# Attention rows: the two halves of the keys added on VectorE before the denominator matmuls, and the output's statistics taken as sums and squares

## The chip, the cores and the metric

The kernel runs on one core of a Trainium2 chip. Each core has a matrix engine (TensorE, PE in the profile, with its weight loads listed as PEld), an elementwise engine (VectorE, DVE), a function engine (ScalarE, ACT), GpSimd (POOL) and a queue for transfers (SyncE, SP). Each engine works through its own list of instructions in order, and they wait for each other through semaphores. SBUF is the working memory, PSUM the memory that TensorE writes to. The metric is the device time of one execution in microseconds (us), the median over runs.

## The reference

The input x is a 256 x 256 image of 128 channels in float32. Four layers follow each other, each of the form x = x + layer(group_norm(x)): triangle attention, a gated recurrence in a transformed space, a triangle product, and a 3 x 3 convolution. The change lies in layer 0 and in the statistics that layer 1 takes of its output. Layer 0, for every image row i, four heads h of 32 channels, and all j, k from 0 to 255:

```
zn = layer_norm(group_norm(x))
q, k, v = zn @ Wq, zn @ Wk, zn @ Wv;   bias = zn @ Wb;   g = sigmoid(zn @ Wg)
scores[i,j,k,h] = q[i,j,h] . k[i,k,h] / sqrt(32) + bias[j,k,h]
a = softmax of scores over k
o[i,j,h] = sum over k of a[i,j,k,h] * v[i,k,h]
x = x + (g * o) @ Wo
```

The group norm of layer 1 needs the mean and the variance of the new x in groups of four channels over the whole image.

## The kernel before

The image lies transposed in HBM, channels on partitions and pixels along the free dimension (`xT`, `x1T`, ...). `transpose_in` makes it, a first pass in `attention` writes the normalised `znT` and the bias, and `attend_bounded` does the attention. (`attend_any` is another branch for weights too large for an unshifted exponential, and isn't taken for these inputs.)

`attend_bounded` has a loop (L603) of 128 rounds, and each round handles two image rows, a = 2 rp and b = 2 rp + 1. The stages are written out in software-pipelined order: while rows a and b are weighted and summed, the scores of rows a+2 and b+2 are made, the projections of the round after next are made, and the output of the round before is finished. Every operation is pinned to the order in which the source calls it, so each engine's queue is the source's order of its own operations. The steps:

- `project` (L494): `ppq`, `ppk`, `ppv`, `ppg` on TensorE, evacuated by ScalarE to `tq`, `tk`, `tg` and by VectorE to `tv`.
- `score` (L514): q times k for one row, keys on partitions, in two halves of 128 keys (`kc`) and four heads, so the scores come as two PSUM tiles `sc` of 128 x 1024 (two heads each). The `sc` tag has two buffers, and one row uses both.
- `biased` (L528): VectorE adds the bias `bT` to one `sc` tile and puts the result in the SBUF tile `e`. This is also what gives the `sc` buffer back.
- `exponent` (L534): ScalarE takes the exponential of `e` in place.
- `values` (L538): TensorE makes the numerators (`nd[:, 0]`, weights `v`) and the denominators (`nd[:, 1]`, weights all ones). Each is a sum over the 256 keys: two accumulating matmuls per head, one for each half. A float32 matmul appears as two records in the profile, so a group of 8 matmuls is 16 records.
- `gated`, `inverse`, `divide` (L549, L555, L560): the denominator is multiplied by 1 + exp(-g) on VectorE (`dn`), inverted on ScalarE by Ln and Exp, and multiplied into the numerator on VectorE (`og`).
- `output` (L568): `px` = Wo times `og` on TensorE; VectorE adds the old x (`xr`) and takes `bn_stats` of the 512 new columns; every second round GpSimd starts the store.

In round 112 `early_statistics` (L115) aggregates the first seven eighths of the statistics, so that `group_affine` (L75) at the head of the recurrence has only the last eighth to aggregate. `group_affine` has a second form, for statistics that are given as sums and as sums of squares about a shift; the triangle stage already uses it. [...]

Of the kernel before, what the change touches and what calls it, by code (L numbers as in the profile page):

```python
# [17 lines left out]
P = 128  # L18
# [12 lines left out]
class Kernel:  # L31
# [245 lines left out]
            W[n] = self.load(pool, I[src], "w2" + n)  # L277
        W["bv"] = self.column(pool, I["L3_conv_bias"], "bv")

    def attention(self, wp, weights, later, xT, x1T, znT, biasD, stats0, stats1):  # L280
        nc, tc, I = self.nc, self.tc, self.i
        w, wb, vb, wo, small = weights
        with ExitStack() as c:
            with ExitStack() as c1:
                ps0 = c1.enter_context(self.pool(name="awq", bufs=2, space=PSUM))
                ab = self.group_affine(wp, ps0, stats0, self.g4, "0")
                lc, cb = self.centering(wp, ps0, ab, "0")

            bias = wp.tile([P, 2, NH, N], F32, name="bias")
# [86 lines left out]
            flag = nc.values_load(small[0:1, 0:1])  # L376
            self.last = {}
            with tc.If(flag > 0) as branch:
                self.attend_bounded(xT, x1T, znT, bias, first, w, wb, vb, wo, stats1)
            self.last = {}  # L380
            with branch.Else():
                self.attend_any(xT, x1T, znT, bias, w, wb, wo, stats1)
            self.last = {}

    def bounded(self, wp, raws, w, wb):
# [64 lines left out]
            V.tensor_copy(fl, top[:, 1:2])  # L450
            return fl

    def attend_bounded(self, xT, x1T, znT, bias, first, w, wb, vb, wo, stats1):


        nc, tc = self.nc, self.tc
# [1 line left out]
        with ExitStack() as c:  # L458
# [17 lines left out]
            pin = lambda f: lambda *a, **k: tc.keep_in_program_order(f(*a, **k))  # L476
            mm, act_t, act_i = pin(self.mm), pin(act), pin(self.act)
            tt, stt, bn = pin(V.tensor_tensor), pin(V.scalar_tensor_tensor), pin(V.bn_stats)
            loaded, t, e, nd, dn, og, x1s = {0: first}, {}, {}, {}, {}, {}, {}

            def chunk(rp):

# [51 lines left out]
            def exponent(i, p2):  # L534
                if 0 <= i < N:
                    act_t(e[i, p2], e[i, p2], AF.Exp, scale=-1.0)

            def values(i):  # L538

                v, r = t[i // 2, "v"], i % 2  # L540
                nd[i] = ps.tile([P, 2, N], F32, name="nd", tag="nd")
                for n in range(2):
                    for kc in range(2):
                        for h in range(NH):
                            hs = slice(h * HD, (h + 1) * HD)
                            lhs = ones if n else v[:, 2 * r + kc, hs]
                            mm(nd[i][hs, n, :], lhs, e[i, h // 2][:, h % 2, kc, :], start=kc == 0, stop=kc == 1)

            def gated(i):  # L549

# [17 lines left out]
            def output(rp):  # L568
                if rp < 0:
                    return  # L570
                xr = chunk(rp)[1]
                if rp % 2 == 0:
                    x1s[rp // 2] = io.tile([P, 1024], F32, name="x1")
                x1 = x1s[rp // 2]
                s = slice((rp % 2) * 512, (rp % 2) * 512 + 512)
                px = ps.tile([P, 512], F32, name="px", tag="pj")
                mm(px, wo["f"], og[rp])
                tt(x1[:, s], px, xr, ALU.add)
                bn(stats1[:, rp, :], x1[:, s])
                if rp % 2 == 1:  # L580
                    nc.gpsimd.dma_start(x1T[:, (rp - 1) * 512:(rp + 1) * 512], x1)

# [18 lines left out]
            for rp in range(N // 2):  # L603
                a, b = 2 * rp, 2 * rp + 1
                score(a + 2)
                inverse(b - 2)
                divide(a - 2)
                biased(a + 2, 0)
                divide(b - 2)
                biased(a + 2, 1)  # L610
                for nm in "qkvg":
                    if nm == "g":
                        exponent(b, 1)
                        exponent(a + 2, 0)
                    project(rp + 2, nm)
                output(rp - 1)
                if rp == N * 7 // 16:
                    self.early_statistics(stats1, "1")
                score(b + 2)
                exponent(a + 2, 1)  # L620
                biased(b + 2, 0)
                exponent(b + 2, 0)
                biased(b + 2, 1)
                values(a)
                gated(a)
                inverse(a)
                values(b)
                gated(b)
            inverse(N - 1)
            divide(N - 2)  # L630
            divide(N - 1)
            output(N // 2 - 1)

    def attend_any(self, xT, x1T, znT, bias, w, wb, wo, stats1):

        nc, tc = self.nc, self.tc
        with ExitStack() as c:
            io = c.enter_context(self.pool(name="a2", bufs=2))
            pj = c.enter_context(self.pool(name="a2w", bufs=2))
            hp = c.enter_context(self.pool(name="a2h", bufs=4))  # L640
            ps = c.enter_context(self.pool(name="a2s", bufs=2, space=PSUM))
            with tc.For_i(0, N // 2) as rp:
                zn = io.tile([P, 512], F32, name="zn2")
                nc.sync.dma_start(zn, znT[:, bass.ds(rp * 512, 512)])
                xr = io.tile([P, 512], F32, name="xr")
                nc.sync.dma_start(xr, xT[:, bass.ds(rp * 512, 512)])
                x1 = io.tile([P, 512], F32, name="x1")
                self.attend(rp, zn, xr, x1, w, wb, wo["h"], bias, pj, hp, ps, stats1)
                nc.sync.dma_start(x1T[:, bass.ds(rp * 512, 512)], x1)
            self.early_statistics(stats1, "1")  # L650

    def attend(self, rp, zn, xr, x1, w, wb, wo, bias, pj, hp, ps, stats1):

# [58 lines left out]
        nc.vector.tensor_tensor(x1, px, xr, ALU.add)  # L712
        nc.vector.bn_stats(stats1[:, bass.ds(rp, 1), :].rearrange("p a b -> p (a b)"), x1)

    def recurrence(self, x1T, x2T, HD_, stats1, stats2, shift2):

# [4 lines left out]
        with ExitStack() as c:  # L723
# [4 lines left out]
            V.tensor_scalar_mul(negid, self.ident, -1.0)  # L728
            gw, gb = {}, {}
            with self.pool(name="rwp", bufs=2, space=PSUM) as ps0:  # L730
                ab, mg, _ = self.group_affine(wp, ps0, stats1, self.g4, "1", True)
                V.tensor_scalar_mul(shift2, mg, -1.0)

                abc = wp.tile([P, 2, 2], F32, name="abc")
                pab = ps0.tile([P, 2, 2], F32, name="pab", tag="gn")
                for half in range(2):
                    for ri in range(2):
                        self.mm(pab[half * HC:(half + 1) * HC, ri, :], self.ident[:, ri * HC:(ri + 1) * HC], ab)
                V.tensor_copy(abc, pab)
                for g, add in (("f", 2.0), ("i", 0.0), ("d", 0.0)):  # L740
                    raw, b0 = W["W" + g], W["b" + g]
                    pb = ps0.tile([P, 2], F32, name="rpb" + g, tag="gn")
                    for half in range(2):
                        hs = slice(half * HC, (half + 1) * HC)
                        for ri in range(2):
                            self.mm(pb[hs, ri:ri + 1], raw[:, ri * HC:(ri + 1) * HC], ab[:, 1:2])
                    gb[g] = wp.tile([P, 2], F32, name="gb" + g)
                    V.scalar_tensor_tensor(gb[g], b0, add, pb, ADD, ADD)
                    gw[g] = wp.tile([P, P], F32, name="gw" + g)
                    V.tensor_scalar_mul(gw[g], raw, ab[:, 0:1])  # L750
# [582 lines left out]
    def run(self, ctx):  # L1333
        nc, tc = self.nc, self.tc
        const = ctx.enter_context(tc.tile_pool(name="const", bufs=1))
        dram = ctx.enter_context(tc.tile_pool(name="dram", bufs=1, space=DRAM))
        image = lambda n: dram.tile([P, NPIX], F32, name=n)
        self.constants(const)
        stats = {n: const.tile([P, NCH, 6], F32, name="stats" + n) for n in "013"}

        stats["2"] = const.tile([P, 2, N // 4], F32, name="stats2")
        shift2 = const.tile([P, 1], F32, name="shift2")
        xT, x1T, x2T, x3T, znT = (image(n) for n in ("xT", "x1T", "x2T", "x3T", "znT"))
        biasD = dram.tile([NH, NPIX], F32, name="biasD")
        HD_ = dram.tile([2, 2 * KS, N, HC], F32, name="HD")
        prodD = image("prodD")
        self.early = {n: [const.tile([P, 2], F32, name=f"early{k}{n}") for k in range(2)] for n in "013"}
        later = ctx.enter_context(self.pool(name="lw", bufs=1))
        with self.pool(name="aw", bufs=1) as wp:
            weights = self.attention_weights(wp)  # L1350
            self.transpose_in(xT, HD_, stats["0"])
            self.attention(wp, weights, later, xT, x1T, znT, biasD, stats["0"], stats["1"])
        self.recurrence(x1T, x2T, HD_, stats["1"], stats["2"], shift2)
        pools = []

        def late():

            if not pools:
                pools.append(ctx.enter_context(self.pool(name="cw", bufs=1, side="right")))
            return pools[0]  # L1360

        self.triangle(x2T, x3T, znT, prodD, stats["2"], shift2, stats["3"], lambda *a: self.transformed_taps(late(), *a))
        self.convolution(x3T, stats["3"], late())
# [58 lines left out]
```

## Time and profile before

The time is 5366.57 us, the median of three runs (5366.4 to 5370.02).

| stretch of the trace, us | what runs | TensorE busy | VectorE busy | ScalarE busy | clock |
|---|---|---|---|---|---|
| 0 to 506 | transposition, first pass of attention | 405.1 | 312.0 | 291.1 | 0.85 |
| 506 to 1882 | `attend_bounded` | 1365.1 | 1040.1 | 959.6 | 0.99 |
| 1882 to 3420 | recurrence | 1472.7 | 1499.4 | 1446.4 | 0.99 |
| 3420 to 5367 | triangle and convolution | 1888.5 | 1154.1 | 882.5 | 0.99 |

Busy time is the time in which an engine had an instruction of its own under way; it says nothing on how well that instruction uses the engine. The clock is the share of full speed that TensorE was granted. An entry such as `[1.22 <-PE px L60]` behind a line of the timeline means that the engine stood idle for 1.22 us before this instruction, and that what it waited for was the write of `px` on TensorE. The trace is in the order of starts; starts of successive instructions on one engine lie closer together than their durations, since they overlap in the pipeline. L60, L54 and L476 are the lines of small helpers which record all matmuls, all activations and the pinned VectorE operations, so the tiles' names tell one from the other.

### The profile page before, as it was taken

How to read it: one execution, taken by the hardware profiler on the slowest of the kernel's cores; microseconds unless marked ns; L12 is line 12 of the kernel's file. 1: busy time of each engine (PE TensorE's matmuls, PEld its weight loads, DVE VectorE, ACT ScalarE, POOL GpSimd, SP SyncE). 2: the span in 40 equal slices, each digit the busy share in tenths (PEclk: the TensorE clock that was granted, in tenths of full speed). 3: DMA queues.
4: the chain of work that ended last, by engine and by line, in shares of the span. 5: the costliest groups of instructions: out<-in, count | busy, mean ns of one | idle time of the engine just before them, and what ended most of it. 6: DMA issues, size and time to landing. Idle time of an engine off the chain costs nothing.

```text
span 5367.2 us, 79719 instructions
## 1 busy us (share of the span) xinstructions
PE 5131.3 (96%) x32117; PEld 2871.9 (54%) x32117; DVE 4005.5 (75%) x5023; ACT 3579.7 (67%) x4923; POOL 267.5 (5%) x488
## 2 busy tenths in 40 slices
PE   5699999999999989999999999899999999999999
PEld 4434555555555533333333333338999954339999
DVE  5666777777777779999999999655334526669886
ACT  4376767777776689999999999784333357772210
POOL 1100000000000000000000000000110010000000
PEclk7799999999999989999999999999999999999999
DMA  8875222222222122222222221577667668864331
GB/s 294 331 267 187 68 80 76 72 80 76 72 76 74 57 76 68 72 68 68 68 72 68 68 68 64 207 283 264 230 234 254 234 248 302 295 228 183 141 130 72
DMA packets 185936, 788.84 MB, mean 147 GB/s; under 512 B 36083, under 2 KB 39432, under 8 KB 136384
## 3 DMA queue, kind: packets, MB, share of 16 engines
q1 hardware_dynamic: 120212, 514.73, 29.3%
q0 software_dynamic: 60416, 268.46, 12.4%
q8 instruction: 256, 4.19, 0.3%
q10 hardware_dynamic: 4936, 0.50, 0.1%
q14 instruction: 116, 0.95, 0.1%
HBM read 512.28 MB, written 271.32 MB: 146 GB/s over the span
## 4 chain that ended last, share of the span: by engine, by line
PE 53%; DVE 31%; issue 11%; ACT 2%; DMA 1%; POOL 1%; POOLq 0%; ACTq 0%; DVEq 0%; SPq 0%
PE z L60 9%; PE nd L60 9%; PE m L60 7%; PE sc L60 5%; PE po L60 4%; PE zc L60 4%; DVE tr L796 3%; DVE t L793 3%; DVE y L793 3%; DVE p L793 3%; DVE yf L793 3%; PE ppv L60 3%; PE ppq L60 3%; PE px L60 3%; PE ppk L60 2%
## 5 line engine op out<-in xcount | busy, mean ns | idle before, releaser
L54 ACT ACTIVATE e<-e 128x1024 f32<-128x1024 f32 x512 | 525.4, 1051 | 195.0 <-DVE e L476 194.7
L476 DVE TENSOR_TENSOR e<-sc,bT 128x1024 f32<-128x1024 f32 x512 | 611.5, 1215 | 39.8 <-PE sc L60 39.8
L956 DVE TENSOR_TENSOR LR<-z,sg 128x512 f32<-128x512 f32 x256 | 268.5, 1050 | 363.3 <-ACT sg L54 358.3
L60 PE MATMUL m<-U,v 128*128 128x128 f32 x4608 | 516.5, 276 | 6.6 <-DVE v L1271 6.6
L60 PEld LDWEIGHTS m<-U,v 128*128 128x128 f32 x4608 | 516.4, 192 | 6.7 <-DVE v L1271 6.7
L60 PE MATMUL z<-wf,zt 128*128 128x128 f32 x4096 | 459.5, 275 | 3.6 <-DVE zn L956 3.6
L60 PEld LDWEIGHTS z<-wf,zt 128*128 128x128 f32 x4096 | 459.3, 192 | 4.6 <-DVE zn L956 4.4
L60 PE MATMUL var<-sq,omat 128*128 128x512 f32 x768 | 360.8, 599 | 1.2 <-ACT rs L54 1.2
L54 ACT ACTIVATE dn<-dn 128x256 f32<-128x256 f32 (+1 forms) x640 | 293.8, 459 | 98.6 <-DVE dn L476 88.5
L54 ACT ACTIVATE sg<-z 128x512 f32<-128x512 f32 x256 | 152.8, 597 | 306.6 <-PE z L60 306.6
L54 ACT ACTIVATE rs<-var,eps 128x1024 f32<-128x1024 f32 x192 | 213.4, 1111 | 168.2 <-PE var L60 168.2
L60 PE MATMUL sc<-tq,tk 32*128 32x256 f32 x4096 | 297.7, 402 | 4.5 <-DVE e L476 4.5
L60 PEld LDWEIGHTS sc<-tq,tk 32*128 32x128 f32 x4096 | 187.0, 185 | 161.0 <-issue 147.2
L60 PE MATMUL nd<-e,tv 128*32 128x256 f32 x4096 | 271.9, 383 | 0.0
L60 PE MATMUL nd<-e,ones 128*32 128x256 f32 x4096 | 268.8, 380 | 0.0
L60 PE MATMUL zc<-xin,lc 128*128 128x512 f32 x512 | 248.8, 610 | 6.1 <-DVE zn L956 5.6
L60 PEld LDWEIGHTS var<-sq,omat 128*128 128x128 f32 x768 | 137.9, 189 | 203.8 <-issue 155.2
L60 PE MATMUL av<-y,ident 128*128 128x512 f32 x384 | 192.2, 609 | 44.1 <-DVE y L793 44.0
L60 PE MATMUL po<-LR 128*128 128x256 f32 x1024 | 222.2, 380 | 7.0 <-DVE LR L956 7.0
L60 PEld LDWEIGHTS po<-LR 128*128 128x128 f32 x1024 | 194.1, 190 | 34.2 <-DVE LR L956 7.7
L1308 ACT COPY m4s<-m 128x512 f32<-128x512 f32 x32 | 18.7, 584 | 285.4 <-PE m L60 285.4
L54 ACT ACTIVATE rs<-rs 128x1024 f32<-128x1024 f32 x192 | 202.9, 1057 | 6.1
(325 smaller groups left out, 10095.0 us busy)
## 6 DMA issues: line engine op xcount, KB each, us to landing
zt<-znT SPq DMA_DIRECT2D x128, 1024.0 KB
znT<-zn POOLq DMA_DIRECT2D x64, 1024.0 KB, 5.7
xin<-x2T SPq DMA_DIRECT2D x64, 1024.0 KB
xr<-x3T SPq DMA_DIRECT2D x46, 768.0 KB
xin<-in_x_dram SPq DMA_DIRECT2D x64, 512.0 KB
xT<-xo POOLq DMA_DIRECT2D x64, 512.0 KB, 10.4
xr<-xT SPq DMA_DIRECT2D x64, 512.0 KB
xin<-xT SPq DMA_DIRECT2D x32, 1024.0 KB
```

The costliest lines, as they stand in the source:

```text
L54: return self.nc.scalar.activation(out, in_, func, bias=bias, scale=scale, **kw)
L60: return self.nc.tensor.matmul(out, lhsT, rhs, start=start, stop=stop)
L476: pin = lambda f: lambda *a, **k: tc.keep_in_program_order(f(*a, **k))
L793: pin(V.tensor_tensor(out, a, b_, op))
L796: pin(V.scalar_tensor_tensor(out, a, k, b_, op0, op1))
L956: pin = lambda f: lambda *a, **k: tc.keep_in_program_order(f(*a, **k))
L1308: nc.scalar.copy(m4, m[4])
```

## The change

The softmax denominator is a sum over all keys. Before, TensorE takes it as two accumulating matmuls with ones for each head. Now VectorE adds the two halves of the keys elementwise (`fold`, a new tile `es` of 128 x 1024 for each row, made by two 128 x 512 adds), and TensorE needs one matmul with ones for each head.

To make room, VectorE loses `bn_stats`: the output add becomes a scalar_tensor_tensor that also writes the sum of its result into `stats1[:, 0]`, and ScalarE writes the sum of squares about a shift (`squares`) into `stats1[:, 1]`. The shift is minus the group mean of x, taken from layer 0's own group norm. `group_affine` uses its second form, and the early aggregate of round 112 is gone. In the loop the two `divide` now follow the two `biased` of row a+2 instead of standing before them. `fold(a)` stands just before the g projection, `fold(b)` after the output of the round before and ahead of the bias adds of row b+2.

```diff
+            def fold(i):
+                x = es[i] = hp.tile([P, NH, N], F32, name="es")
+                for p2 in range(2):
+                    y = e[i, p2]
+                    tt(x[:, 2 * p2:2 * p2 + 2], y[:, :, 0, :], y[:, :, 1, :], ALU.add)
...
             def values(i):
-                for n in range(2):
-                    for kc in range(2):
-                        for h in range(NH):
-                            hs = slice(h * HD, (h + 1) * HD)
-                            lhs = ones if n else v[:, 2 * r + kc, hs]
-                            mm(nd[i][hs, n, :], lhs, e[i, h // 2][:, h % 2, kc, :], start=kc == 0, stop=kc == 1)
+                for kc in range(2):
+                    for h in range(NH):
+                        hs = slice(h * HD, (h + 1) * HD)
+                        mm(nd[i][hs, 0, :], v[:, 2 * r + kc, hs], e[i, h // 2][:, h % 2, kc, :], start=kc == 0, stop=kc == 1)
+                folded = i in es
+                for kc in range(1 if folded else 2):
+                    for h in range(NH):
+                        hs = slice(h * HD, (h + 1) * HD)
+                        mm(nd[i][hs, 1, :], ones, es[i][:, h] if folded else e[i, h // 2][:, h % 2, kc, :],
+                           start=kc == 0, stop=folded or kc == 1)
...
-                tt(x1[:, s], px, xr, ALU.add)
-                bn(stats1[:, rp, :], x1[:, s])
+                stt(x1[:, s], px, 1.0, xr, ALU.mult, ALU.add, accum_out=stats1[:, 0, rp:rp + 1])
...
+            def squares(rp):
+                if rp >= 0:
+                    junk = hp.tile([P, 512], F32, name="junk", bufs=1)
+                    s = slice((rp % 2) * 512, (rp % 2) * 512 + 512)
+                    act_t(junk, x1s[rp // 2][:, s], AF.Square, bias=shift1, accum_out=stats1[:, 1, rp:rp + 1])
...
                 inverse(b - 2)
+                biased(a + 2, 0)
                 divide(a - 2)
-                biased(a + 2, 0)
+                biased(a + 2, 1)
                 divide(b - 2)
-                biased(a + 2, 1)
                 for nm in "qkvg":
                     if nm == "g":
+                        fold(a)
                         exponent(b, 1)
                         exponent(a + 2, 0)
                     project(rp + 2, nm)
                 output(rp - 1)
-                if rp == N * 7 // 16:
-                    self.early_statistics(stats1, "1")
                 score(b + 2)
                 exponent(a + 2, 1)
+                squares(rp - 1)
+                fold(b)
                 biased(b + 2, 0)
...
-                ab, mg, _ = self.group_affine(wp, ps0, stats1, self.g4, "1", True)
+                ab, mg, _ = self.group_affine(wp, ps0, stats1, self.g4, "1", True, shift=shift1)
...
-        stats = {n: const.tile([P, NCH, 6], F32, name="stats" + n) for n in "013"}
+        stats = {n: const.tile([P, NCH, 6], F32, name="stats" + n) for n in "03"}
+        stats["1"] = const.tile([P, 2, N // 2], F32, name="stats1")
+        shift1 = const.tile([P, 1], F32, name="shift1")
```

More of the change, by code (lines that the diff above doesn't have):

```diff
@@ L278, in later_weights, with attention @@
         W["bv"] = self.column(pool, I["L3_conv_bias"], "bv")
-    def attention(self, wp, weights, later, xT, x1T, znT, biasD, stats0, stats1):
+    def attention(self, wp, weights, later, xT, x1T, znT, biasD, stats0, stats1, shift1):
         nc, tc, I = self.nc, self.tc, self.i
@@ L285, in attention @@
                 ps0 = c1.enter_context(self.pool(name="awq", bufs=2, space=PSUM))
-                ab = self.group_affine(wp, ps0, stats0, self.g4, "0")
+                ab, mg, _ = self.group_affine(wp, ps0, stats0, self.g4, "0", True)
+                nc.vector.tensor_scalar_mul(shift1, mg, -1.0)
                 lc, cb = self.centering(wp, ps0, ab, "0")
@@ L378, in attention @@
             with tc.If(flag > 0) as branch:
-                self.attend_bounded(xT, x1T, znT, bias, first, w, wb, vb, wo, stats1)
+                self.attend_bounded(xT, x1T, znT, bias, first, w, wb, vb, wo, stats1, shift1)
             self.last = {}
             with branch.Else():
-                self.attend_any(xT, x1T, znT, bias, w, wb, wo, stats1)
+                self.attend_any(xT, x1T, znT, bias, w, wb, wo, stats1, shift1)
             self.last = {}
@@ L451, in bounded, with attend_bounded @@
             return fl
-    def attend_bounded(self, xT, x1T, znT, bias, first, w, wb, vb, wo, stats1):
+    def attend_bounded(self, xT, x1T, znT, bias, first, w, wb, vb, wo, stats1, shift1):
         nc, tc = self.nc, self.tc
@@ L478, in attend_bounded @@
             tt, stt, bn = pin(V.tensor_tensor), pin(V.scalar_tensor_tensor), pin(V.bn_stats)
-            loaded, t, e, nd, dn, og, x1s = {0: first}, {}, {}, {}, {}, {}, {}
+            loaded, t, e, es, nd, dn, og, x1s = {0: first}, {}, {}, {}, {}, {}, {}, {}
             def chunk(rp):
@@ L632, in attend_bounded, with attend_any @@
             output(N // 2 - 1)
-    def attend_any(self, xT, x1T, znT, bias, w, wb, wo, stats1):
+            squares(N // 2 - 1)
+    def attend_any(self, xT, x1T, znT, bias, w, wb, wo, stats1, shift1):
         nc, tc = self.nc, self.tc
@@ L640, in attend_any @@
             hp = c.enter_context(self.pool(name="a2h", bufs=4))
+            cp = c.enter_context(self.pool(name="g0", bufs=1))
+            parts = cp.tile([P, N // 2, 6], F32, name="parts")
+            mv, m2 = cp.tile([P, 2], F32, name="mvany"), cp.tile([P, 1], F32, name="m2any")
             ps = c.enter_context(self.pool(name="a2s", bufs=2, space=PSUM))
@@ L647, in attend_any @@
                 x1 = io.tile([P, 512], F32, name="x1")
-                self.attend(rp, zn, xr, x1, w, wb, wo["h"], bias, pj, hp, ps, stats1)
+                self.attend(rp, zn, xr, x1, w, wb, wo["h"], bias, pj, hp, ps, parts)
                 nc.sync.dma_start(x1T[:, bass.ds(rp * 512, 512)], x1)
-            self.early_statistics(stats1, "1")
+            V = nc.vector
+            V.bn_aggr(mv, parts)
+            V.tensor_tensor(m2, mv[:, 0:1], shift1, ALU.add)
+            V.scalar_tensor_tensor(mv[:, 1:2], m2, m2, mv[:, 1:2], ALU.mult, ALU.add)
+            V.memset(stats1, 0.0)
+            V.tensor_scalar_mul(stats1[:, :, 0], mv, float(NPIX))
     def attend(self, rp, zn, xr, x1, w, wb, wo, bias, pj, hp, ps, stats1):
@@ L713, in attend, with recurrence @@
         nc.vector.bn_stats(stats1[:, bass.ds(rp, 1), :].rearrange("p a b -> p (a b)"), x1)
-    def recurrence(self, x1T, x2T, HD_, stats1, stats2, shift2):
+    def recurrence(self, x1T, x2T, HD_, stats1, shift1, stats2, shift2):
         nc, tc, I = self.nc, self.tc, self.i
@@ L1346, in run @@
         prodD = image("prodD")
-        self.early = {n: [const.tile([P, 2], F32, name=f"early{k}{n}") for k in range(2)] for n in "013"}
+        self.early = {n: [const.tile([P, 2], F32, name=f"early{k}{n}") for k in range(2)] for n in "03"}
         later = ctx.enter_context(self.pool(name="lw", bufs=1))
@@ L1351, in run @@
             self.transpose_in(xT, HD_, stats["0"])
-            self.attention(wp, weights, later, xT, x1T, znT, biasD, stats["0"], stats["1"])
-        self.recurrence(x1T, x2T, HD_, stats["1"], stats["2"], shift2)
+            self.attention(wp, weights, later, xT, x1T, znT, biasD, stats["0"], stats["1"], shift1)
+        self.recurrence(x1T, x2T, HD_, stats["1"], shift1, stats["2"], shift2)
         pools = []
```

## The prediction

> **What bounds the kernel now.** I first read the page's 40 slices for the stage (attention is 506 to 1882 us of the trace), then the table of windows for a stretch inside it.
>
> ```profile
> 1000.00:1500.00 500.00, 500.00 (x5264) 262.38 (x5263) 380.59 (x518) 352.95 (x518) 12.28 (x23) 1.00 0.24 75
> ```
>
> In 500 us TensorE (the column after the length) is busy for 500, VectorE (the third busy column) for 380.6, ScalarE (the fourth) for 353, at full clock (1.00). The chain of waits of one loop round, two rows of attention, shows TensorE alone:
>
> ```profile
> 1201.58 1.08 PE sc L60 x16
> 1202.65 3.59 PE nd L60 x64
> 1206.24 1.08 PE sc L60 x16
> 1207.32 1.05 PE ppq L60 x2
> 1208.37 0.86 PE ppk L60 x2
> 1209.23 1.08 PE ppv L60 x8
> 1210.31 0.86 PE ppg L60 x2
> 1211.17 1.05 PE px L60 x2
> ```
>
> The sum is 10.64 us, and the `bn_stats` that ends each round's output starts 10.641 to 10.646 us after the one before for all rounds but the last three and one in the middle. The timeline of VectorE over the first part of the round:
>
> ```profile
> 1201.61 0.69 DVE L476 TENSOR_TENSOR x<-px,xr 128x512 f32<-128x512 f32 x1 [1.22 <-PE px L60]
> 1202.34 0.69 DVE L476 BATCH_NORM_STATS2 stats<-x 128x6 f32<-128x512 f32 x1
> 1202.95 2.34 DVE L476 TENSOR_TENSOR e<-sc,bT 128x1024 f32<-128x1024 f32 x2
> 1205.20 0.41 DVE L476 SCALAR_TENSOR_TENSOR dn<-tg,nd 128x256 f32<-128x256 f32 x1
> 1206.31 0.42 DVE L476 SCALAR_TENSOR_TENSOR dn<-tg,nd 128x256 f32<-128x256 f32 x1 [0.69 <-PE nd L60]
> ```
>
> The bias adds of row b+2 end at 1205.29, and the next round's `score` starts on TensorE at 1206.24. `score` needs both `sc` tiles back from those adds (two buffers, two used per row). So VectorE has only 0.95 us of slack here, though it idles 2.5 us in a round (1.22 for `px`, 0.69 for `nd`, 0.31 for `ppv`, 0.29 for `sc`). The odd round in the middle, with the early aggregate of L119, takes 16.24 us and shows what happens when the slack is used up:
>
> ```profile
> 1713.97 3.19 DVE L119 BATCH_NORM_AGGREGATE early<-stats 128x2 f32<-128x672 f32 x1
> 1717.27 2.35 DVE L476 TENSOR_TENSOR e<-sc,bT 128x1024 f32<-128x1024 f32 x2
> 1718.54 0.70 PE L60 MATMUL sc<-tq,tk 32*128 32x256 f32 x4 [1.40 <-DVE e L476]
> 1719.67 2.08 PE L60 MATMUL sc<-tq,tk 32*128 32x256 f32 x12 [0.43 <-DVE e L476]
> ...
> 1720.00:1723.00 3.00, 3.00 (x14) 1.67 (x11) 2.40 (x5) 1.53 (x4) 0.00 (x0) 0.50 0.00 0
> ```
>
> Four matmuls of `score` go after the first add, the other twelve only 0.05 us after the second. After these pauses (1.40 and 0.43 us) the clock stood at 0.50.
>
> **What the Trainium skill says.** (1) "VectorE: DVE Perf Modes", the perf-mode tier table: an fp32 `tensor_tensor` is held to one element a cycle. The trace agrees: 512-wide ones with both inputs in SBUF start 0.60 us apart:
>
> ```profile
> 2505.34 0.73 DVE L793 TENSOR_TENSOR s<-mag,inv 128x512 f32<-128x512 f32 x1
> 2505.95 0.73 DVE L793 TENSOR_TENSOR u<-u,tr 128x512 f32<-128x512 f32 x1
> ```
>
> (2) The same page, "Two Vector instructions with no wait between them": an operation that writes an accumulator out is two instructions. VectorE has none in this trace; ScalarE has, with a read instruction behind:
>
> ```profile
> 2507.19 1.15 ACT L54 ACTIVATE x2q<-x,shift 128x1024 f32<-128x1024 f32 x1
> 2508.23 0.20 ACT L54 ACTIVATION_READ_ACCUMULATOR x2q<-x,shift 128x1 f32 x1
> 2508.45 0.63 ACT L54 ACTIVATE tq<-tr 128x512 f32<-128x512 f32 x1
> ```
>
> (3) "TensorEngine Tiling (Array Packing)", Key Properties: a change of tiling mode drains TensorE. In the chain the same 512-wide projection costs 1.05 us after `sc` but 0.86 in a run of its own kind, so 0.19 a change, which halving `nd` does not remove. (4) "TensorE: Matmul & The Clock Gate", HAM oscillation, warns of idle gaps above about 3.4 us. Here less was enough, as shown; but the recurrence stage pauses 0.6 to 0.9 us once per 23.3 us at clock 1.00 throughout.
>
> **The change, part by part.** *Folded ones.* `nd` is four groups of 16 records, each four waves of 0.213 us (2 x 2 groups: values and ones for two rows): 4 x 0.853 + 0.19 = 3.6. Folding leaves 8 records for each ones group: 2 x 0.427 = **0.853 us less TensorE work a round**, to 9.79.
>
> *Four adds on VectorE*, 128x512, SBUF to SBUF: 4 x 0.60 = 2.40 us. The two of row a come after `tv` (start about 1210.4, spacing 0.6) and fall in the 1.22 us in which VectorE waits for `px`: 1.20 in 1.22, hidden. The two of row b stand between the output add and the bias adds of b+2: 1.20 us in the stretch with the slack. They take the place of `bn_stats`.
>
> *Statistics.* `bn_stats` goes (0.61 to the next start). The output add becomes a scalar_tensor_tensor with a sum beside it: same 0.60 spacing, plus the accumulator read. From below this is 0 (no extra instruction); from above 0.25, as on ScalarE (there 2508.45 - 2507.19 = 1.26 against 0.96 spacing, 0.3, less the pointer bias). The one-column operations on VectorE start 0.07 to 0.16 apart (L84 to L101); I take 0.12.
>
> *Squares on ScalarE*: by half the 1024-wide row above, 1.26 - 0.43 = 0.83 us a round. ScalarE goes from 7.5 to 8.3 of a round. It stands after `exponent`(a+2, 1), which ends about 1.4 us after `px`; the next, `exponent`(b+2, 0), then waits for its bias add until 3.2. 1.4 + 0.83 = 2.2: hidden. Behind it `inverse` and `tq` run as now.
>
> *Moved divides.* They follow the bias adds, so `biased`(a+2, 0) no longer queues behind a wait for ScalarE's inverse. `px` has its divide 1.2 us early: nothing. The extra affine columns and memory changes are one-off, tenths of a us. The end of the stage: add, squares, reduce (about 1.7 us to the group matmul) against add, `bn_stats`, aggregate (1.67 measured): nothing.
>
> *The early aggregate is removed*: 16.24 - 10.64 = **5.6 us saved**, once.
>
> **The new round.** Take `px`'s end as 0. VectorE: start 0.03, output add 0.60, accumulator 0.12, two folds 1.20, first bias add 1.125 (half of 1205.20 - 1202.95), second 1.215 to its end, release 0.05: 4.34. TensorE is free at 1.08 + 3.59 - 0.85 = 3.82, so **`score` now waits 0.5 us** for its second tile, the wait of the L119 round made small. Behind it in TensorE's queue stands the whole rest: `score` 1.08 (four waves whether or not four records ran ahead; in the L119 round twelve still took four), then 1.05 + 0.86 + 1.08 + 0.86 + 1.05, in all 5.98, to the next `px` end. Round: 4.34 + 5.98 = 10.32, closed, since the next output add waits for that `px`. Does VectorE get there? Second bias add's issue done 4.2, `gated` twice 4.87, `score` tile ready about 5.1, adds and divides 2 x (1.125 + 0.335) to 8.0, `tv` waits for `ppv` to 8.44, folds from 9.04 to 10.24: 0.1 before `px`. Yes, barely. Saving 10.644 - 10.32 = 0.32 for some 125 steady rounds, 40.6 us, plus 5.6: **46 us, to 5320**.
>
> **Rivals.** *A, TensorE stays the bound* (bias adds return in time): 0.853 x 125 + 5.6 = 112, so 5254. For it: VectorE's spacings sum to only 9.5 in a round. Against: the slack of 0.95 less the 0.85 that TensorE gains leaves 0.1, and the folds with the accumulator exceed `bn_stats` by 0.7. *B, no change:* accumulator and extra semaphores cost 0.4 in that stretch, round 10.6, 5356 to 5372. *C, slower:* the sum runs at half rate (0.53 more, plus a 0.16 read: round 10.89), +31 - 5.6, so 5392; a pause beyond 1 us might also bring the clock down, as it did in the L119 round, and then several hundred us are possible. Against: a half-us pause did not do it in the recurrence, and `px` lies in PSUM, so the add has only one SBUF input.
>
> **Numbers.** Main case 0.70 (accumulator 0 to 0.25: 5305 to 5337, a little further with odd waits), A 0.08, B 0.08, C 0.14. Range 5283 to 5366: A lies mostly below, C above. Faster by over 0.2% (below 5356): 0.79; within: 0.07; slower: 0.14.
>
> **What would show it.** A round of 10.2 to 10.45; `nd` in ones at half its count; TensorE busy about 95% in the stretch with one pause, `sc` waiting for `e` in every round; VectorE near 9.3 of a round; the `px` wait before the output add shrunk from 1.22 to about 0.1; clock 1.00; no 16 us round. Wrong if `sc` waits for nothing (A), if the output add's spacing exceeds 0.9 us (B, C), or if the clock shows 0.50 in the rounds (C).

## The result, and the profile after

The changed kernel takes 5322.6 us (median of four runs, 5321.14 to 5326.74) against 5368.3 us for the kernel before on the same chip: a ratio of 0.9916, 95% interval 0.9898 to 0.9933. That is 46 us less (36 to 55 us by the interval). The forecast was 5320 us and 46 us.

The chain of waits of the changed kernel over one round (start, length, what):

```profile
1202.26 1.08 PE sc L60 x16
1203.33 2.73 PE nd L60 x48
1206.06 1.59 PE sc L60 x16
1207.65 1.05 PE ppq L60 x2
```

`nd` fell from 3.59 to 2.73 us (64 records to 48). But the second `sc` of the round rose from 1.08 to 1.59: TensorE gains 0.86 us and gives 0.51 back. The waits say what it gives it to. The first line is from the table of waits for 1000 to 1500 us (what waited, for what; total, times, longest), the second is one of these waits in the timeline:

```profile
PEld sc L60 <- DVE e L477: 11.2, 49, 0.2
1206.52 0.73 PEld L60 LDWEIGHTS sc<-tq,tk 32*128 32x128 f32 x12 [0.23 <-DVE e L477]
```

These are 49 waits, one in each round; the kernel before had none of them in this stretch. Only the weight loads' idle time is listed. The four records (two matmuls) of `score` that went ahead cover the rest of the pause, so TensorE's busy time does not show it. The stretch still reads as TensorE fully busy (the first busy column), while VectorE, the third, went from 380.6 to 472.6 of 500:

```profile
1000.00:1500.00 500.00, 500.00 (x4643) 259.48 (x4640) 472.60 (x729) 393.96 (x633) 12.78 (x24) 1.00 0.25 78
```

VectorE's timeline through the stretch that the prediction rests on, from `tv` of one round to `gated` of rows a and b:

```profile
1200.38 0.69 DVE L477 TENSOR_TENSOR tv<-ppv,vb 128x512 f32<-128x512 f32 x1 [0.36 <-PE ppv L60]
1200.99 1.28 DVE L477 TENSOR_TENSOR es<-e 128x512 f32<-128x512 f32 x2
1202.29 0.69 DVE L477 SCALAR_TENSOR_TENSOR x<-px,xr 128x512 f32<-128x512 f32 x1
1202.91 0.08 DVE L477 DVE_READ_ACCUMULATOR x<-px,xr 128x1 f32 x1
1202.91 1.29 DVE L477 TENSOR_TENSOR es<-e 128x512 f32<-128x512 f32 x2
1204.12 2.35 DVE L477 TENSOR_TENSOR e<-sc,bT 128x1024 f32<-128x1024 f32 x2
1206.38 0.74 DVE L477 SCALAR_TENSOR_TENSOR dn<-tg,nd 128x256 f32<-128x256 f32 x2
```

The folds of row a (1200.99) lie in the old 1.22 us wait for `px`, and the output add now starts without a wait. The folds of row b (1202.91) stand ahead of the bias adds. These end at 1206.47, and the twelve blocked `sc` records get their first weights at 1206.52. The median round in the trace (from one `gated` of row b to the next) is 10.296 us against 10.644, and no long round stands out any more.

### The profile page after: what moved, and what is told of

Same layout as the page of the kernel before. It is cut to its first block, busy times and chain, and to the rows that moved or that the text cites. A ratio compares the mean times of both kernels' runs of the same rounds, so it can differ in the third digit from the quotient of the medians.

```text
span 5319.6 us, 76896 instructions
## 1 busy us (share of the span) xinstructions
PE 5079.0 (95%) x30069; PEld 2836.1 (53%) x30069; DVE 4210.7 (79%) x5534; ACT 3655.6 (69%) x5179; POOL 266.7 (5%) x488
## 4 chain that ended last, share of the span: by engine, by line
PE 52%; DVE 31%; issue 12%; ACT 2%; DMA 1%; POOL 1%; POOLq 0%; ACTq 0%; SPq 0%; DVEq 0%
PE z L60 9%; PE m L60 7%; PE nd L60 6%; PE sc L60 6%; PE po L60 4%; PE zc L60 3%; DVE tr L824 3%; DVE t L821 3%; DVE y L821 3%; DVE p L821 3%; DVE yf L821 3%; PE ppv L60 3%; PE ppq L60 3%; PE px L60 3%; PE ppk L60 2%
## 5 line engine op out<-in xcount | busy, mean ns | idle before, releaser
L60 PE MATMUL sc<-tq,tk 32*128 32x256 f32 x4096 | 361.4, 408 | 3.3 <-DVE e L477 3.3
L477 DVE TENSOR_TENSOR es<-e 128x512 f32<-128x512 f32 x512 | 329.1, 684 | 0.0
L60 PEld LDWEIGHTS sc<-tq,tk 32*128 32x128 f32 x4096 | 220.8, 184 | 190.6 <-issue 147.9
L54 ACT ACTIVATE dn<-dn 128x256 f32<-128x256 f32 (+1 forms) x640 | 279.8, 456 | 61.6 <-DVE dn L477 51.3
```

The source lines that it names most:

```text
L54: return self.nc.scalar.activation(out, in_, func, bias=bias, scale=scale, **kw)
L60: return self.nc.tensor.matmul(out, lhsT, rhs, start=start, stop=stop)
```

## The experiments

Two theories. **The closed round** (the prediction's): `px`, output add, folds of b, two bias adds, `score` and the projections up to the next `px` make a loop, and only what stands in it costs. **VectorE's total** (the rival): VectorE has become so full that its sum of work sets the round. Times are medians; rounds are medians in the trace of each run. The kernel before took 5369 to 5370 us beside these runs.

**One row at a time.** Each run drops one `fold`.

```diff
 # fold_a_only
                 squares(rp - 1)
-                fold(b)
                 biased(b + 2, 0)
 # fold_b_only
                     if nm == "g":
-                        fold(a)
                         exponent(b, 1)
```

> The changed kernel with only row a of each pair folded; row b's denominator again takes two matmuls per head. Theory (the round is closed by the stretch px, output add, folds of b, two bias adds, score): without the folds of b the stretch ends at 0.03 + 0.62 + 2.35 + 0.05 = 3.05 us after px, TensorE is free only at 4.24, so score does not wait and the round is TensorE's own, 10.644 - 0.427 = 10.22 us, shorter than with both rows folded (10.30): 5312 us. Rival (VectorE's total work sets the round): also 10.22, but then folding b alone gives the same.

> The changed kernel with only row b folded. Theory: the stretch keeps its 4.26 us after px, TensorE is free at 4.24, so the round is about 10.28 to 10.30 us, score waits for the bias add by a few hundredths, and the time is that of both rows folded, 5319 to 5323 us, though VectorE has 1.2 us less to do. Rival (VectorE's total): VectorE has as little to do as with row a alone, so 10.22 us and 5312 us as there.

Measured: row a alone 5313.5 us (ratio 0.9896, 0.9881 to 0.9911), round 10.212; row b alone 5326.7 us (0.992, 0.9906 to 0.9933), round 10.300. In both kernels TensorE has the same work to do, and so has VectorE. The chains, first of row a alone, then of row b alone:

```profile
1209.89 3.16 PE nd L60 x56
1213.04 1.08 PE sc L60 x16
```

```profile
1204.96 3.16 PE nd L60 x56
1208.12 1.16 PE sc L60 x16
```

`nd` is the same 3.16; `sc` stretches only where row b is folded. And with row b alone VectorE is not full at all: it waits for `px` before every output add, as in the kernel before:

```profile
DVE x L477 <- PE px L60: 58.4, 48, 1.2
```

So its total cannot set this round. The place of the two adds does. It also follows that folding the second row, as the change does, makes the round longer (10.296) than folding row a alone (10.212). The time of row b alone lies above the 5319 to 5323 us expected. In its trace the loop is 2.9 us longer than that of the change, and 2.2 of these lie in the interval before the last (12.54 us against 10.35).

**The statistics alone.** No `fold`, everything else as changed.

> The changed kernel with no row folded: only the statistics (sums beside the output add, squares on ScalarE, no early aggregate) and the moved divides. Theory: TensorE's 10.644 us round is unchanged, the 16.24 us round is gone: 5368 - 5.6 = 5362 us, all rounds equal. Rival (the squares or the sums cost time in each round): a round above 10.65.

Measured: 5368.0 us, ratio 1.000 (0.9992 to 1.0008), no difference that can be seen. The 5362 us expected lie outside this interval. The steady round is 10.644, so sums and squares cost nothing there, and the 16 us round is gone. In the trace the loop (first to last `gated` of row b) is only 2.6 us shorter, not 5.6: the interval before the last is 11.63 us instead of 8.60. There TensorE's `px` waits for the last divide, and the clock is lower after it. The same `px` in the kernel before, then with the statistics alone:

```profile
1863.82 1.12 PE L60 MATMUL px<-og,wo 128*128 128x512 f32 x2 [1.65 <-DVE og L476]
```

```profile
1858.68 1.98 PE L60 MATMUL px<-og,wo 128*128 128x512 f32 x2 [3.11 <-DVE og L477]
```

Of these 3.03 us, 1.46 are the longer wait: behind `score` the last divide now follows two bias adds and a divide, where before it followed one bias add, and one bias add and one divide are 1.13 and 0.33 us from start to start. The other 1.57 are `px` itself (1.98 against 1.12) and the `score` behind it (1.92 against 1.21), at a clock of 0.54 from 1858.6 to 1861 us; at the same `px` of the kernel before it was 1.00. This is read from one trace of each kernel, and whether the longer wait brought the clock down was not tested.

**The divides back in their old place.**

```diff
+                divide(a - 2)
                 biased(a + 2, 0)
-                divide(a - 2)
+                divide(b - 2)
                 biased(a + 2, 1)
-                divide(b - 2)
```

> The changed kernel with the two divides back ahead of the bias adds of row a+2. Expected: the steady round stays at 10.30 us or rises by up to 0.1 (the first divide waits for ScalarE's inverse, and the bias adds of a+2 with it, into the 0.36 us wait before tv); the last two rounds, where px waits for the divides, become up to 3 us shorter, as the run with the statistics alone suggests. So 5320 us if the round stays; 5330 us if it rises by 0.1.

Measured: 5321.5 us (0.9914, 0.9897 to 0.993), round 10.296. VectorE waits 0.60 us for ScalarE's inverse and no longer waits ahead of `tv`: one wait for another. The `px` of the round without projections waits 2.01 us in place of 2.75 in the changed kernel, and that interval is 9.56 us in place of 10.35. Together with the last interval (6.18 against 6.02) this is 0.6 us, where up to 3 us were expected. A microsecond is below what the times resolve, so the move of the divides is nil in the rounds, and at the loop's end its cost is seen in the traces only.

**The same needless add in two places.** A 128x256 add with nobody waiting for its result:

```diff
 # more_in_stretch
                 fold(b)
+                w_(256)
                 biased(b + 2, 0)
 # more_before_v
                 divide(b - 2)
+                w_(256)
                 for nm in "qkvg":
```

> The changed kernel with one needless add (128x256, both inputs in SBUF, 0.335 us from start to start) on VectorE between the folds of b and the bias adds of b+2. Theory (closed round through that stretch): every round 0.335 us longer, 10.63 us, 5365 us. Rival (VectorE's total, which has 0.54 us of waits a round): the waits absorb it, 5322 to 5327 us.

> The same needless add, placed instead after the last divide and ahead of tv, where VectorE waits 0.36 us for ppv. Theory: hidden in that wait, round 10.30 us, 5323 us. Rival (any work added to VectorE counts): as much as in the other place.

Measured: in the stretch 5367.9 us (0.9998, 0.9989 to 1.0007), round 10.629, that is 0.333 more, nearly the add's full 0.335. Ahead of `tv`: 5324.6 us (0.9919, 0.9903 to 0.9936), round 10.296, unchanged, though VectorE is busier there (488.8 us of 500). A third of a microsecond per round in the wrong place uses up the whole gain of the change. TensorE in the slower of the two:

```profile
1206.71 0.70 PE L60 MATMUL sc<-tq,tk 32*128 32x256 f32 x4
1207.57 1.13 PE L60 MATMUL sc<-tq,tk 32*128 32x256 f32 x12 [0.17 <-DVE e L479]
```

The pause is now long enough to show as idle behind the first four records.

**A large dose**, two adds of 128x1024 in the stretch, for the clock.

> The changed kernel with two needless 128x1024 adds (2.25 us) between the folds of b and the bias adds of b+2, so that score pauses about 1.5 and 0.4 us in each round, as in the round with the aggregate of the kernel before. If the clock holds: round 10.30 + 2.25 = 12.55 us and 5604 us. If such pauses bring the clock down as in that round, up to 3 us more a round: 5600 to 5980 us, and the clock of the stage below 0.9.

Measured, in a single run: 5870.2 us. The first two rounds are 12.69 us, then the rounds lie between 14.15 and 15.81 us up to the loop's end. TensorE in one of them, and the table of windows for 600 to 1400 us, with the clock of 0.85 near the end of its line:

```profile
1200.48 0.70 PE L60 MATMUL sc<-tq,tk 32*128 32x256 f32 x4 [1.72 <-DVE e L479]
1201.62 1.13 PE L60 MATMUL sc<-tq,tk 32*128 32x256 f32 x12 [0.43 <-DVE e L479]
1202.68 2.07 PE L60 MATMUL ppq<-zn,wq 128*128 128x512 f32 x2
```

```profile
600.00:1400.00 800.00, 683.07 (x5220) 346.20 (x5224) 660.29 (x930) 445.13 (x713) 14.39 (x27) 0.85 0.18 54
```

From the third round on, with pauses of 1.72 and 0.43 us in each, the clock is at half for part of the time (`ppq` takes 2.07 us, not 1.1). The changed kernel's half microsecond stays clear of this, at 1.00, and so does the pause that the 128x256 add in the stretch made a third of a microsecond longer.

**The sum left out.** This kernel does not take the sum of the new x; its column of the statistics stays zero.

```diff
-                stt(x1[:, s], px, 1.0, xr, ALU.mult, ALU.add, accum_out=stats1[:, 0, rp:rp + 1])
+                tt(x1[:, s], px, xr, ALU.add)
```

> The changed kernel with the output add as a plain add; the sum of the new x is left out (its column of the statistics is zero). The trace of the changed kernel has the accumulator read of 0.08 us start together with the next fold, 0.62 us after the add, against 0.60 for two such adds: so the sum should cost 0.02 us a round, 2.5 us in all, 5320 us, round 10.28 us. Had it cost the 0.12 us that the prediction took: round 10.18 us, 5308 us.

Measured: 5320.4 us (0.9906, 0.9889 to 0.9922), round 10.281. The sum costs 0.015 us a round, about 2 us in all by the rounds.

**The output add taken out of the loop.** If the closed round is right, the bias adds of row b+2 should not stand behind the output add. Only a later `ppk` needs the buffer of `px` back (the projections and `px` share two buffers, and `ppk` is the second tile after `px`). On VectorE the order of the folds and the bias adds stays; without the add between them, the folds of row b no longer wait for `px`. The squares come one round later.

```diff
+                fold(b)
                 output(rp - 1)          # px alone
                 score(b + 2)
                 exponent(a + 2, 1)
-                squares(rp - 1)
-                fold(b)
+                squares(rp - 2)
                 biased(b + 2, 0)
...
                 gated(b)
+                add(rp - 1)             # the output add and the store
```

> Both rows folded, with the order on VectorE changed: folds of b ahead of the output add's place (they wait for nothing there), bias adds of b+2 next, the output add after gated(b), and the squares one round later. Theory: bias adds now follow score alone, the second ends about 3.5 us after px, before TensorE is free at 3.8, so score waits for nothing and the round is TensorE's 10.644 - 0.853 = 9.79 us: about 5255 us. Rival (VectorE's total, 9.43 us of starts plus 0.54 us of waits that stay): 9.97 us, about 5280 us; or no gain on 10.30 if VectorE is the bound already.

Measured: 5261.3 us, ratio 0.9798 (0.9785 to 0.9811), round 9.779: 61 us below the change (and 108 below the kernel before beside it), with the same work on every engine. (About 5255 us were expected; in the trace the interval before the last reads 12.00 us.) The chain:

```profile
1203.06 1.08 PE sc L60 x16
1204.14 2.73 PE nd L60 x48
1206.87 1.08 PE sc L60 x16
```

`sc` is back at 1.08 and the full 0.86 of `nd` is kept. VectorE does in 9.78 us what it did in 10.30, so its total did not set the round of the change. But now both engines are full (TensorE 500, VectorE 496.7 of 500 us):

```profile
1000.00:1500.00 500.00, 500.00 (x4924) 259.21 (x4916) 496.72 (x768) 414.27 (x664) 13.84 (x26) 1.00 0.27 83
```

To see whether VectorE has become a second bound, the needless 128x256 add of before was put ahead of `tv` here, the place where it was free in the change.

> The version with the late output add, with the needless 128x256 add ahead of tv. In that version VectorE is busy for 496.7 of 500 us, so it should have no place left to hide work: if VectorE's total is now a second bound, every round grows by nearly the 0.335 us, 10.05 to 10.1 us, 5295 to 5305 us; if TensorE alone still bounds, 5261 to 5266 us.

Measured: 5291.9 us (0.9854, 0.9838 to 0.9871), round 10.042: 0.263 of the 0.335 us come through. VectorE is busy for 496.7 of 500 us as before, TensorE only for 490.7. The chain of waits now goes over VectorE (`waste` is the needless add):

```profile
1212.08 0.34 DVE waste L478
1212.41 0.61 DVE tv L478
1213.02 0.04 issue
1213.07 1.13 PE px L60 x2
```

`px` takes the buffer of `ppv`, which `tv` gives back, so a later `tv` holds TensorE up. VectorE's work now counts in a place where it did not count in the change. Whether its total sets this round or this second loop through `tv`, the run cannot tell, since VectorE has hardly any idle time left.

## Why the prediction was right

- **Folded ones, 0.853 us less on TensorE.** `nd` went from 3.59 to 2.73 us, 0.86.
- **The new wait of 0.5 us.** `sc` went from 1.08 to 1.59, 0.51. The two places of the needless add show that it depends on what stands in that stretch.
- **The round of 10.32 us.** 10.296, closer than its terms. The accumulator read, for which 0.12 was taken between 0 and 0.25, cost 0.015 by the run without the sum; ScalarE's separate read was a poor neighbour to price it by. So from `px`'s end to the release of the second tile it took 4.26 us (1202.26 to 1206.52) and not 4.34. Against that, what was left of `score` took 1.13 us (to 1207.65) and not 1.08. Two errors partly cancel, which is luck.
- **Folds of row a hidden.** Yes: they fill the old wait for `px`; folding row a alone reaches 10.212, the 10.22 expected of TensorE alone, and leaving them out (row b alone, 10.300) does not shorten the round of the change.
- **Squares hidden on ScalarE, 0.83 us.** ScalarE's busy share went from 353 to 394 us of 500, by the round 7.5 to 8.1 us, and the round did not move in the run with the statistics alone.
- **The early aggregate, 5.6 us once.** The long round is gone, but the run with the statistics alone could not be told from the kernel before: in its trace 3.0 us were lost again in the interval before the last. The term that the prediction put at nothing, "the end of the stage" and "moved divides", was mis-sized for the rounds without projections, where `px` waits for the divides. The prediction looked at the last statistics alone (from the end of the last output add to the matmul of the group means: 1.56 us against 1.67 before). In the changed kernel `px` waits 2.75 us there, against 1.65, and the interval reads 10.35 us against 8.60; the last interval, 6.02 against 8.33, makes up for it. Over the runs with changed statistics (the large dose apart) the interval before the last varies from 9.25 to 12.54 us.
- **The total.** 125 steady rounds gave 43.5 us where 40.6 were forecast, and the long round 5.6. In the two traces the loop is 49.6 us shorter and the whole execution 47.6. The times say 46 us with an interval from 36 to 55, so that 46 came out as 46 is closer than the measurement can tell.
- **What would show it.** Two signs failed. "TensorE busy about 95%" reads 100%, because the records of the matmuls that went ahead cover the pause; the length of `sc` in the chain was the place to look. VectorE, "near 9.3 of a round", was busy for 9.7 us of 10.3 (472.6 of 500). The rest was seen.
- **Rivals.** A (5254 us) was turned down for the reason that the runs confirm; with the output add out of the loop it comes true, at 5261. B and C needed the output add with its sum to cost 0.4 us and more above the plain one; it takes 0.62 us to the next start, against 0.60 without the sum.
- **A reading that does not hold.** The prediction takes 0.19 us for a change of tiling mode from a projection of 1.05 us behind `sc` against 0.86 behind its own kind. But in its own chain `px` also takes 1.05 us, right behind `ppg`, so these lines do not show that price. The 0.853 us saved do not depend on it.

## What to carry to other kernels

Where two engines hand buffers to each other in a loop, add up the loop from release to release: work taken off the busiest engine is worth only as much as the slack that is left on the buffer that it needs next. Ahead of adding work to the second engine, ask which of its places lie outside that loop; here the same 0.335 us cost 43 us in one place and nothing that could be seen in another. And if an operation in the loop has no one waiting for it, such as the output add, move it behind the ones that release buffers: on top of this change that was worth more (61 us) than the change itself (46).

## What the runs showed of the hardware that was not expected

- A VectorE add that also writes its sum has a second instruction in the trace (0.08 us), which starts with the next operation; leaving the sum out made the round 0.015 us shorter. On ScalarE the read behind the squares is a record of 0.19 us; what it costs was not tried.
- Pauses of TensorE of 0.5 us in each 10.3 us round leave the clock at 1.00, and so do some 0.84 us (an estimate, 0.51 + 0.333) in each 10.6 us round with the 128x256 add in the stretch. With pauses of 1.72 and 0.43 us in each round the first two rounds, 12.69 us long, are at full clock; from the third on it is halved for part of the time, and its mean over 600 to 1400 us is 0.85. Where between these the limit lies was not tried.
- A group of matmuls that stops half way for a buffer can read as busy throughout: 500 of 500 us with half a microsecond of waiting in each round.
